# Order of the first loads, of the row statistics and of the bias product at the start of a four-layer attention kernel

## The chip, the cores and the metric

The kernel runs on one core of a Trainium2 chip. A core has a matrix engine (TensorE, PE in the profile, with its weight loads as PEld), a vector engine (VectorE, DVE), a scalar engine (ScalarE, ACT), GpSimd (POOL) and SyncE (SP), which here only issues DMAs. The metric is the device time of one execution in microseconds. The kernel before took 3056.87 us, the median of 3 runs (3055.58 to 3056.94).

## What is computed

The reference chains four layers, each a cross attention and a feed-forward part, over x (16 batches of 256 rows and 256 columns) and a context of the same shape. Only the first attention matters here:

```
def _L0_xattn_ref(query, key, value, w_q, w_k, w_v, w_o, b_q, b_k, b_v, b_o):
    q = split_heads(query @ w_q.T + b_q)
    k = split_heads(key @ w_k.T + b_k)
    v = split_heads(value @ w_v.T + b_v)
    scores = jnp.einsum('bhqd,bhkd->bhqk', q, k) / scale
    attn = jax.nn.softmax(scores, axis=-1)
    ctx = jnp.einsum('bhqk,bhkd->bhqd', attn, v)
    return ctx.transpose(0, 2, 1, 3).reshape(B, -1, D_MODEL) @ w_o.T + b_o
...
x = x + _L0_xattn_ref(_layernorm(x, axis=-1), ctx_1024, ctx_1024, ...)
x = x + _L0_ffn_ref(_layernorm(x, axis=-1), ...)
```

There are 16 heads of 16 columns. Queries come from the normalised x, keys and values from the context. The feed-forward part of this layer rounds its three weight matrices to -1, 0 and 1 after it divided them by the mean of their absolute values, so all of a matrix must have been read before it can be rounded.

## The kernel before

**Start.** x is kept in the core's memory, one tile of 128 x 2 x 256 for each batch. Lines 81 and 82 issue its 16 loads on SP. Lines 142 to 144 take the mean and the variance of every row of all 16 batches (`tile_stats`, L113 and L114, two row tiles for each batch). Then `load_pack` loads the pack w_l0a of the attention in eight parts (L99) in the order of SPECS: wq, wk, bq, bk, wv, bv, wo, bo; and the pack w_l0f of the feed-forward part in three parts of 1 MB.

**narrow_attention** serves layer 0 and layer 3. For layer 0 it first makes the reciprocal roots of all rows at once: `inv_std` (L122), a Sqrt on ScalarE and a reciprocal on VectorE, with a load of the Sqrt table, and then the table of logarithm and exponential for the rest (L172). It makes the masks (L182 to L197), clears buffers (L208), and turns the value bias into a term of the output (L211 to L221): two transposes, a copy, four matmuls with wo, and an addition into bo. That sum, `add_bias`, is added to x on GpSimd when a batch enters (L237).

**One batch.** `context` loads the transposed context (cT, 256 KB, three buffers). `values` makes the values (L290), `project` keys and queries (L261), each with a second copy by `rest_of` (L283). `enter` normalises x (L129), `turn` transposes it (L247). Batch 0 does all this before the loop. The loop then has eight half steps for each batch: in each, two heads' pairs of scores (L446 into s_ps), their row maxima on VectorE (L321), and seven half steps later the same products the other way round (t_ps), their exponentials on ScalarE (L349) and the weighted sums (L361). s_ps has three buffers and each half step takes two, so the maxima decide when TensorE can go on. The stages of the next batch are spread over these half steps: context and enter at h = 0, turn at 1, queries at 2 and 3, keys at 4 and 5, values at 7. Batches two back are divided (L379 to L387) and leave (L407, L414), with new statistics and row extremes (L538).

**Beside the loop.** `beside` calls the generator `weights` once for each half step from batch 1 on: twelve reductions of w_l0f (L502), their total (L508 to L514), then twelve steps that round it (L519 and L520 on VectorE, L521 on GpSimd). At half step 4 of batches 8, 9 and 10 it loads the packs of later layers.

**Order.** Each engine runs its instructions in a fixed order, but this order isn't simply that of the text. When the program is built, a planner takes the written order as priority and puts instructions whose inputs it reckons to be ready into holes of their engine. `issue_after` keeps ScalarE's work behind the table load. `rsqrt` (L683 to L695) is the other way to a reciprocal root: one GpSimd operation, Ln and Exp on ScalarE, and four GpSimd operations.

Of the kernel before, what the change touches and what calls it, by code (L numbers as in the profile page):

```python
# [9 lines left out]
F32 = mybir.dt.float32  # L10
# [8 lines left out]
B = 16  # L19
# [6 lines left out]

SPECS = {
    "w_l0a": [
        ("wq", 128, (2, 256)), ("wk", 128, (2, 256)), ("bq", 128, (2,)), ("bk", 128, (2,)),
        ("wv", 128, (2, 256)), ("bv", 128, (256,)), ("wo", 128, (2, 256)), ("bo", 128, (256,)),  # L30
    ],
    "w_l0f": [("wg", 128, (2, 1024)), ("wu", 128, (2, 1024)), ("wd", 128, (8, 256))],
    "w_l1a": [("gk", 128, (6, 8)), ("gb", 128, (8,)), ("os", 128, (256,))],
# [24 lines left out]
def kernel(ctx: ExitStack, tc: tile.TileContext, a: dict, out: bass.AP):  # L58
# [19 lines left out]
    nc.gpsimd.memset(eps6, 1e-6)  # L78

    X = [xp.tile([P, 2, D], F32, name=f"x{b}") for b in range(B)]  # L80
    for b in range(B):
        nc.sync.dma_start(X[b], x_v[b])

    def pool(stack, name, bufs, space=None, side=None):
        kw = {} if space is None else {"space": space}
# [31 lines left out]
        for t in range(2):  # L117
            tile_stats(mv, 2 * b + t, X[b][:, t, :])

    root = []  # L120

    def inv_std(mv):  # L122
        r = stat.tile([P, NT], F32, tag="rstd", name="rstd")
        root[:] = [nc.scalar.activation(r, mv[:, :, 1], AF.Sqrt, bias=eps5)]
        nc.vector.reciprocal(r, r)
        return r

    def normalize(dst, src, mv, r, i):
        nc.vector.tensor_scalar(dst, src, mv[:, i, 0:1], r[:, i : i + 1], ALU.subtract, ALU.mult)  # L129

# [8 lines left out]
                nc.tensor.transpose(pt[:, c, t * P : (t + 1) * P], xn[:, t, c * P : (c + 1) * P], ident)  # L139
        nc.scalar.copy(dst[:, :, dst_off : dst_off + S], pt)  # L140

    mv = new_stats()
    for b in range(B):
        batch_stats(mv, b)

    def bcast_max(col, wk, ps):

        t1 = ps.tile([1, P], F32, tag="misc", name="gm_ps")
# [7 lines left out]
        return m  # L156


    def narrow_attention(tag, w, mv, q_bias=None, k_bias=None, v_bias=None, add_bias=None,
                         new=None, rstd=None, wk=None, ps=None, before=None, between=None, beside=None, left=None, one_set=False):  # L160

        SCALE = 0.25
        with ExitStack() as st:
            one = pool(st, f"{tag}one", 1)
            if rstd is None:
                new = new_stats()
                rstd = inv_std(mv)
                if one_set:  # L170
                    with tc.issue_after(root[0].ins):
                        tables = nc.scalar.preload_act_table_set("natural_log_exp_and_others")  # L172
                    st.enter_context(tc.issue_after(tables.ins))
                wk = pool(st, f"{tag}wk", 2)
                ps = pool(st, f"{tag}ps", 2, PSUM)


            i32 = ident.rearrange("p (a b) -> p a b", b=32)
# [29 lines left out]
                nc.gpsimd.memset(t, 0.0)  # L208
            for t in vals:
                nc.gpsimd.memset(t[:, :, :, 16:17], 1.0)  # L210
            if v_bias is not None:  # L211

                bT = one.tile([P, 2, P], F32, name="bT")
                pb = ps.tile([P, 2, P], F32, tag="misc", name="bT_ps")
                for c in range(2):
                    nc.tensor.transpose(pb[:, c, :], v_bias[:, c * P : (c + 1) * P], ident)
                nc.vector.tensor_copy(bT, pb)
                pb = ps.tile([P, D], F32, tag="misc", name="bo_ps")
                for c in range(2):
                    nc.tensor.matmul(pb, lhsT=bT[:, c, :], rhs=w["wo"][:, c, :], start=(c == 0), stop=(c == 1))  # L220
                nc.vector.tensor_tensor(add_bias, pb, add_bias, ALU.add)  # L221

            state = {}

            def context(b):
                cT = wk.tile([P, 2, S], F32, tag="cT", name="cT", bufs=3)
                nc.sync.dma_start(cT, ctxT_v[b])
                state[b] = dict(cT=cT, v=vals[b % 3])

            def enter(b):  # L230

                xn = wk.tile([P, 2, D], F32, tag="xn", name="xn", bufs=3)
                for t in range(2):
                    normalize(xn[:, t, :], X[b][:, t, :], mv, rstd, 2 * b + t)
                if add_bias is not None:
                    for t in range(2):
                        nc.gpsimd.tensor_tensor(X[b][:, t, :], X[b][:, t, :], add_bias, ALU.add)  # L237
                state[b]["xn"] = xn

            def turn(b):  # L240
                s = state[b]
# [42 lines left out]

            def values(b):
                s = state[b]
                pv = ps.tile([P, 2, D], F32, tag="misc", name="v_ps")
                for t in range(2):
                    for c in range(2):
                        nc.tensor.matmul(  # L290
                            pv[:, t, :],
                            lhsT=s["cT"][:, c, t * P : (t + 1) * P],
                            rhs=w["wv"][:, c, :],
                            start=(c == 0),
                            stop=(c == 1),
                        )
                for par in range(2):
                    d_ = s["v"][:, :, :, 32 * par : 32 * par + 16].rearrange("p t h d -> p (t h) d")
                    s_ = pv.rearrange("p t (h x) -> p (t h) x", x=32)[:, :, 16 * par : 16 * par + 16]
                    nc.scalar.copy(d_, s_)  # L300
# [115 lines left out]
                if left is not None:  # L416
                    left(b, new)

            context(0)
            values(0)  # L420
            project(0, "k")
            rest_of(0, "k")
# [3 lines left out]
            turn(0)  # L426
            project(0, "q")
            rest_of(0, "q")
            if between is not None:
                between()  # L430

# [2 lines left out]
            for i in range(halves + (16 if beside is None else 40)):  # L434
                b, h = divmod(i, 8)
                made, flipped = [], []
                if i < halves:
                    made = score_mms(i // 2, i % 2)
                if 0 <= i - LAG < halves:
                    flipped = flipped_mms((i - LAG) // 2, (i - LAG) % 2)  # L440

                lists = [m for pair in zip(made, flipped) for m in pair] if made and flipped else made + flipped
                for t in range(2):
                    for _, _, mms in lists:
                        out_, l_, r_ = mms[t]
                        nc.tensor.matmul(out_, lhsT=l_, rhs=r_, start=True, stop=True)  # L446
                if made:
                    maxima(i // 2, made)
                if h == 5 and b + 1 < B:
                    rest_of(b + 1, "k")  # L450
                if flipped:
                    exps((i - LAG) // 2, flipped)
                if h % 4 == 1 and 5 <= i <= halves + 1:
                    top_rows(i // 4 - 1)
                if h % 2 == 0 and 0 <= i - LAG - 3 < halves:
                    weigh((i - LAG - 3) // 2)

                if b + 1 < B:
                    if h == 0:
                        context(b + 1)  # L460
                        enter(b + 1)
                    elif h == 1:
                        turn(b + 1)
                    elif h == 2:
                        project(b + 1, "q")
                    elif h == 3:
                        rest_of(b + 1, "q")
                    elif h == 4:
                        project(b + 1, "k")
                    elif h == 7:  # L470
                        values(b + 1)
                if h == 2 and 2 <= b <= B + 1:
                    divide(b - 2, 1)
                elif h == 3 and 2 <= b <= B + 1:
                    back(b - 2, 1)
                elif h == 6 and 2 <= b <= B + 1:
                    leave(b - 2)
                elif h == 5 and 1 <= b <= B:
                    divide(b - 1, 0)
                elif h == 7 and 1 <= b <= B:  # L480
                    back(b - 1, 0)
                if beside is not None:
                    beside(b, h, ps)
        return new


    def l0_attn(mv, w, w_f, qp, load):
        q = dict(
            wg=qp.tile([P, 2, 1024], BF16, name="l0g"), wu=qp.tile([P, 2, 1024], BF16, name="l0u"),
            wd=qp.tile([P, 8, 256], BF16, name="l0d"), deq=qp.tile([P, 3], F32, name="l0deq"),  # L490
# [5 lines left out]

        def weights(ps):

            tot = qp.tile([P, 3, 4], F32, name="l0tot")
            for j, n in enumerate(names):  # L500
                for c in range(4):
# [24 lines left out]
        def beside(b, h, ps):  # L526
            if not made:
                made.append(weights(ps))
            if h == 4 and 8 <= b < 11:
                load(("w_l1a", "w_l1f", "w_l2a")[b - 8])  # L530
            if b >= 1:
                next(made[0], None)

        def left(b, new):
# [23 lines left out]

        with ExitStack() as st:
            sp = pool(st, "l0sp", 2)  # L560
            mv = narrow_attention(
                "l0a", w, mv, q_bias=w["bq"], k_bias=w["bk"], v_bias=w["bv"], add_bias=w["bo"], beside=beside, left=left,
                one_set=True,
            )
            for _ in made[0]:
                pass
        return mv, q
# [1396 lines left out]
    with ExitStack() as st:  # L1964
        keep = pool(st, "l3keep", 1)
        dram = pool(st, "l3dram", 1, bass.MemoryType.DRAM)
        with ExitStack() as s2:
            qp = pool(s2, "l2fq", 1)
            with ExitStack() as s1:
# [2 lines left out]
                pq = pool(s_q, "l0fq", 1, side="right")  # L1972
                with ExitStack() as s0:
                    pf, pa = pool(s0, "l0fw", 1), pool(s0, "l0aw", 1)
                    wa = load_pack(pa, "w_l0a")
                    wf = load_pack(pf, "w_l0f")
                    mv, q0 = l0_attn(mv, wa, wf, pq, lambda n: packs.update({n: load_pack(pw, n, lambda z: not late(z))}))
                mv, q2 = layers_1_2(q0, s_q, qp, packs)
            xs, acc, wm, g = layers_2_3(mv, q2, keep, dram)
        l3_ffn(xs, acc, wm, g)  # L1980
# [112 lines left out]
```

## Time and profile before

| what | value |
|---|---|
| median of 3 runs | 3056.87 us |
| profiled execution, its own time | 3063.33 us |
| its span | 3061.6 us |
| TensorE busy | 2792.1 us (91%) |
| VectorE busy | 1751.6 us (57%) |
| ScalarE busy | 1282.2 us (42%) |
| GpSimd busy | 973.6 us (32%) |
| mean granted TensorE clock | 0.954 |
| first 20 us: busy TensorE, VectorE | 0.66 us, 14.62 us |
| 20 to 40 us: busy TensorE, VectorE | 11.87 us, 12.79 us |
| DMA in the first 40 us | 299 and 258 GB/s |

Times in the profile's rows count from the start of the span. A row of the chain of waits gives start, length, and engine, tile and line; it follows the work that ended last back to the start. A row of the timeline gives start, length, engine, line, operation, the tile written and the tiles read, and the count. A row of the table of stages gives the length of a stage and then each engine's busy time and count, the granted clock as a share of full speed, the busy share of the DMA engines and what they moved. A busy TensorE isn't one at its peak: a matmul at half the clock counts as longer.

### The profile page before, as it was taken

How to read it: one execution, taken by the hardware profiler on the slowest of the kernel's cores; microseconds unless marked ns; L12 is line 12 of the kernel's file. 1: busy time of each engine (PE TensorE's matmuls, PEld its weight loads, DVE VectorE, ACT ScalarE, POOL GpSimd, SP SyncE). 2: the span in 40 equal slices, each digit the busy share in tenths (PEclk: the TensorE clock that was granted, in tenths of full speed). 3: DMA queues.
4: the chain of work that ended last, by engine and by line, in shares of the span. 5: the costliest groups of instructions: out<-in, count | busy, mean ns of one | idle time of the engine just before them, and what ended most of it. 6: DMA issues, size and time to landing. Idle time of an engine off the chain costs nothing.

```text
span 3061.6 us, 49389 instructions
## 1 busy us (share of the span) xinstructions
PE 2792.1 (91%) x18661; PEld 1983.1 (65%) x18683; DVE 1751.6 (57%) x4397; ACT 1282.2 (42%) x3293; POOL 973.6 (32%) x1944
## 2 busy tenths in 40 slices
PE   5899998787999999999999998698999959999996
PEld 4566664445666666666666664355666648888885
DVE  6777676894555555555555666987777561222221
ACT  2455556664444444444444445534555531111110
POOL 1100003453433344433443333321010034555552
PEclk9899998888999999999999999889999979999998
DMA  5000000000000000000000000411010035676764
GB/s 181 15 12 12 19 1 1 15 1 31 11 11 11 11 11 11 11 11 11 11 11 5 15 18 27 155 65 44 29 32 29 22 114 170 209 216 208 215 211 118
DMA packets 81772, 177.09 MB, mean 58 GB/s; under 512 B 25935, under 2 KB 50526, under 8 KB 70590
## 3 DMA queue, kind: packets, MB, share of 16 engines
q0 software_dynamic: 24864, 105.69, 11.4%
q1 hardware_dynamic: 56670, 68.25, 7.1%
q8 instruction: 147, 2.41, 0.3%
q14 instruction: 91, 0.75, 0.1%
HBM read 147.04 MB, written 31.06 MB: 58 GB/s over the span
## 4 chain that ended last, share of the span: by engine, by line
PE 75%; DVE 11%; POOL 5%; issue 4%; ACT 3%; DMA 1%; POOLq 0%; SPq 0%; DVEq 0%; ACTq 0%
PE h_ps L1883 8%; PE o_ps L1905 8%; PE s_ps L446 7%; PE qk_ps L1038 6%; PE acc_ps L361 4%; PE acc_ps L1177 4%; PE qk_ps L261 4%; PE out_ps L1098 4%; PE s_ps L1119 3%; PE eT_ps L1161 3%; PE v_ps L1054 3%; PE t_ps L446 2%; PE v_ps L290 2%; PE out_ps L407 2%; DVE low L1128 1%
## 5 line engine op out<-in xcount | busy, mean ns | idle before, releaser
L349 ACT ACTIVATE e<-t_ps 128x512 f32<-128x512 f32 x512 | 278.2, 594 | 228.5 <-PE t_ps L446 207.4
L321 DVE TENSOR_REDUCE top<-s_ps 128x2 f32<-128x512 f32 x512 | 330.7, 682 | 50.5 <-PE t_ps L446 43.6
L1138 ACT ACTIVATE e<-s_ps,low 128x256 f32<-128x256 f32 x512 | 236.2, 472 | 288.4 <-DVE low L1128 287.8
L1149 POOL TENSOR_SCALAR e<-e,total 128x256 f32<-128x256 f32 x512 | 238.4, 485 | 325.2 <-DVE total L1146 227.4
L446 PE MATMUL s_ps<-k,q 32*128 32x256 f32 x2048 | 332.0, 411 | 10.1 <-DVE top L321 9.9
L446 PE MATMUL t_ps<-q,k 32*128 32x256 f32 x2048 | 337.4, 409 | 2.7 <-ACT e L349 2.6
L1883 PE MATMUL h_ps<-xgT,w 128*128 128x256 f32 (+1 forms) x1248 | 254.7, 362 | 0.0
L1905 PE MATMUL o_ps<-w,h 128*128 128x256 f32 x1136 | 251.6, 379 | 0.0
L446 PEld LDWEIGHTS s_ps<-k,q 32*128 32x128 f32 x2048 | 197.8, 188 | 82.7 <-issue 35.7
L1128 DVE TENSOR_REDUCE low<-s_ps 128x2 f32<-128x512 f32 x256 | 164.3, 683 | 134.7 <-PE s_ps L1119 134.7
L1883 PEld LDWEIGHTS h_ps<-xgT,w 128*128 128x128 f32 x1248 | 222.1, 192 | 27.6 <-ACT xgT L1872 0.2
L1905 PEld LDWEIGHTS o_ps<-w,h 128*128 128x128 f32 x1136 | 212.9, 190 | 27.4
L446 PEld LDWEIGHTS t_ps<-q,k 32*128 32x128 f32 x2048 | 206.0, 187 | 20.3 <-ACT e L349 14.0
L1895 ACT ACTIVATE h<-h_ps,w 128x256 f32<-128x256 f32 (+1 forms) x156 | 62.5, 451 | 370.9 <-PE h_ps L1883 361.8
L1177 PE MATMUL acc_ps<-eT,v 128*64 128x256 f32 x1024 | 172.4, 397 | 38.5 <-DVE eT L1164 38.4
L1164 DVE COPY eT<-eT_ps 128x512 f32<-128x512 f32 x256 | 165.2, 678 | 19.4 <-PE eT_ps L1161 19.3
L1893 DVE TENSOR_SCALAR h<-h_ps,w 128x256 f32<-128x256 f32 (+1 forms) x156 | 64.5, 455 | 179.1 <-PE h_ps L1883 121.2
L1915 DVE TENSOR_TENSOR y<-o_ps,w 128x256 f32<-128x256 f32 x71 | 27.1, 420 | 226.3 <-PE o_ps L1905 226.3
L1177 PEld LDWEIGHTS acc_ps<-eT,v 128*64 128x64 f32 x1024 | 70.6, 136 | 124.3 <-DVE eT L1164 67.4
L1119 PE MATMUL s_ps<-k,q 64*128 64x256 f32 x1024 | 148.3, 404 | 0.0
L361 PE MATMUL acc_ps<-e,vals 128*32 128x256 f32 x2048 | 143.6, 393 | 0.0
L1161 PE MATMUL eT_ps<-ident,e 128*128 128x128 f32 x1024 | 143.1, 285 | 0.0
(477 smaller groups left out, 5605.2 us busy)
## 6 DMA issues: line engine op xcount, KB each, us to landing
cT<-in_ctxT_dram SPq DMA_DIRECT2D x32, 256.0 KB, 2.7
away<-h SPq DMA_DIRECT2D x30, 256.0 KB, 2.0
h<-away SPq DMA_DIRECT2D x30, 256.0 KB, 3.7
x<-in_x_dram SPq DMA_DIRECT2D x16, 256.0 KB, 5.9
w_l2a<-in_w_l2a_dram SPq DMA_DIRECT2D x4, 1024.0 KB, 7.0
va<-in_ctx_dram SPq DMA_DIRECT2D x32, 128.0 KB, 2.9
c1T<-in_ctxT_dram SPq DMA_DIRECT2D x16, 256.0 KB, 2.6
c2T<-in_ctxT_dram SPq DMA_DIRECT2D x16, 256.0 KB, 2.7
```

Source lines behind the costliest of these rows:

```text
L321: nc.vector.tensor_reduce(top[:, :, col], sp, AX.X, ALU.max)
L349: nc.scalar.activation(e, tp, AF.Exp)
L361: nc.tensor.matmul(acc[32 * j : 32 * j + 32, par, :], lhsT=s["v"][:, k, 4 * g + j, 16 * par : 16 * par + 32], rhs=es[j][:, k, :], start=(k ...
L446: nc.tensor.matmul(out_, lhsT=l_, rhs=r_, start=True, stop=True)
L1119: nc.tensor.matmul(sp[j][:, t, :], lhsT=q[rows, g % 2, t * P : (t + 1) * P], rhs=k[rows, g % 2, :], start=True, stop=True,)
L1128: nc.vector.tensor_reduce(low[:, :, j], sp[j], AX.X, ALU.max, negate=True)
L1138: nc.scalar.activation(es[j][:, t, :], sp[j][:, t, :], AF.Exp, bias=low[:, t, j : j + 1], accum_out=total[:, t, j : j + 1])
L1149: nc.gpsimd.tensor_scalar(es[j][:, t, :], es[j][:, t, :], total[:, t, j : j + 1], 1.0, ALU.mult, ALU.mult)
L1161: nc.tensor.transpose(pt[:, k, t * P : (t + 1) * P], es[j][:, t, k * P : (k + 1) * P], ident)
L1177: nc.tensor.matmul(s["acc"][64 * j : 64 * j + 64, g % 2, :], lhsT=s["v"][g // 4][:, k, (2 * (g % 4) + j) * 64 : (2 * (g % 4) + j + 1) * 64 ...
L1883: nc.tensor.matmul(pp[:, f - f0, cols_], lhsT=w1[:, c * 1024 + f * P : c * 1024 + (f + 1) * P], rhs=xT[:, c, cols_], start=(c == 0), stop= ...
L1905: nc.tensor.matmul(pp[:, j, :], lhsT=h[:, f, j * P : (j + 1) * P], rhs=w2[:, f * D : (f + 1) * D], start=(f == 0), stop=(f == 7),)
```

## The change

SPECS holds w_l0a in another order. Before the loop of x loads there is now only x0; `narrow_attention` loads the first context block, then (through a function that it is handed) the pack w_l0a, then x1 to x15. Statistics of batch 0 are taken alone and its root is made by `rsqrt`; the Sqrt, its table and the reciprocal are gone. Batch 1 has its statistics and root ahead of the loop, and half step i of the loop takes those of batch i + 2; roots follow for batches 2 and 3, 4 to 9, and 10 to 15. The bias product stands behind the queries of batch 0, and `add_bias` is added to the x of batch 0 behind it. The pack w_l0f is loaded by the generator `weights` at half step 7 of batch 0. Layer 3 calls the same function; there only its first context load stands earlier in the text.

```diff
-        ("wq", 128, (2, 256)), ("wk", 128, (2, 256)), ("bq", 128, (2,)), ("bk", 128, (2,)),
-        ("wv", 128, (2, 256)), ("bv", 128, (256,)), ("wo", 128, (2, 256)), ("bo", 128, (256,)),
+        ("wv", 128, (2, 256)), ("wk", 128, (2, 256)), ("bk", 128, (2,)), ("wq", 128, (2, 256)), ("bq", 128, (2,)),
+        ("bv", 128, (256,)), ("wo", 128, (2, 256)), ("bo", 128, (256,)),
...
-    for b in range(B):
+    def load_x(b):
         nc.sync.dma_start(X[b], x_v[b])
+    load_x(0)
...
-    mv = new_stats()
-    for b in range(B):
-        batch_stats(mv, b)
...
-                new = new_stats()
-                rstd = inv_std(mv)
-                if one_set:
-                    with tc.issue_after(root[0].ins):
-                        tables = nc.scalar.preload_act_table_set("natural_log_exp_and_others")
-                    st.enter_context(tc.issue_after(tables.ins))
+                new, mv = new_stats(), new_stats()
+                rstd = stat.tile([P, NT], F32, tag="rstd", name="rstd")
+                tables = nc.scalar.preload_act_table_set("natural_log_exp_and_others")
+                st.enter_context(tc.issue_after(tables.ins))
...
+            def roots(lo, hi):
+                cols = slice(2 * lo, 2 * hi)
+                rsqrt(wk, rstd[:, cols], mv[:, cols, 1], ALU.add, 1.0, 1e-5)
+
+            context(0)
+            if fresh:
+                w = w()
+                q_bias, k_bias, v_bias, add_bias = (w[n] for n in ("bq", "bk", "bv", "bo"))
+                for b in range(1, B):
+                    load_x(b)
+                batch_stats(mv, 0)
+                roots(0, 1)
...
             project(0, "q")
             rest_of(0, "q")
+            if v_bias is not None:
...
+            biased(0)
+            if fresh:
+                batch_stats(mv, 1)
+                roots(1, 2)
...
+                if fresh and i + 2 < B:
+                    batch_stats(mv, i + 2)
+                    for lo, hi in ((2, 4), (4, 10), (10, B)):
+                        if i + 3 == hi:
+                            roots(lo, hi)
...
         def weights(ps):
+            w_f.update(load("w_l0f"))
+            yield
...
-            if b >= 1:
+            if b >= 1 or h == 7:
                 next(made[0], None)
```

The lines behind `if v_bias is not None` are those of L211 to L221, unchanged.

More of the change, by code (lines that the diff above doesn't have):

```diff
@@ L118, in batch_stats @@
             tile_stats(mv, 2 * b + t, X[b][:, t, :])
[L120 to L126, printed above, removed]
     def normalize(dst, src, mv, r, i):
@@ L156, in bcast_max, with narrow_attention @@
         return m
-    def narrow_attention(tag, w, mv, q_bias=None, k_bias=None, v_bias=None, add_bias=None,
-                         new=None, rstd=None, wk=None, ps=None, before=None, between=None, beside=None, left=None, one_set=False):
+    def narrow_attention(tag, w, mv, new=None, rstd=None, wk=None, ps=None, before=None, between=None, beside=None, left=None):
         SCALE = 0.25
@@ L166, in narrow_attention, with context @@
             one = pool(st, f"{tag}one", 1)
-            if rstd is None:
-                new = new_stats()
-                rstd = inv_std(mv)
-                if one_set:
-                    with tc.issue_after(root[0].ins):
-                        tables = nc.scalar.preload_act_table_set("natural_log_exp_and_others")
-                    st.enter_context(tc.issue_after(tables.ins))
+            q_bias = k_bias = v_bias = add_bias = None
+            fresh, state = rstd is None, {}
+            if fresh:
[3 more added lines that the diff above has]
+                st.enter_context(tc.issue_after(tables.ins))
                 wk = pool(st, f"{tag}wk", 2)
                 ps = pool(st, f"{tag}ps", 2, PSUM)
+            def context(b):
+                cT = wk.tile([P, 2, S], F32, tag="cT", name="cT", bufs=3)
+                nc.sync.dma_start(cT, ctxT_v[b])
+                state[b] = dict(cT=cT)
+            def roots(lo, hi):
[9 more added lines that the diff above has]
+                roots(0, 1)
             i32 = ident.rearrange("p (a b) -> p a b", b=32)
@@ L210, in narrow_attention @@
                 nc.gpsimd.memset(t[:, :, :, 16:17], 1.0)
[L211 to L228, printed above, removed]
             def enter(b):
@@ L234, in enter, with biased @@
                     normalize(xn[:, t, :], X[b][:, t, :], mv, rstd, 2 * b + t)
+                if b:
+                    biased(b)
+                state[b]["xn"] = xn
+            def biased(b):
                 if add_bias is not None:
@@ L237, in enter @@
                         nc.gpsimd.tensor_tensor(X[b][:, t, :], X[b][:, t, :], add_bias, ALU.add)
-                state[b]["xn"] = xn
             def turn(b):
@@ L286, in values @@
                 s = state[b]
+                s["v"] = vals[b % 3]
                 pv = ps.tile([P, 2, D], F32, tag="misc", name="v_ps")
@@ L417, in leave @@
                     left(b, new)
-            context(0)
             values(0)
@@ L428, in narrow_attention @@
             rest_of(0, "q")
+            if v_bias is not None:
+                bT = one.tile([P, 2, P], F32, name="bT")
+                pb = ps.tile([P, 2, P], F32, tag="misc", name="bT_ps")
+                for c in range(2):
+                    nc.tensor.transpose(pb[:, c, :], v_bias[:, c * P : (c + 1) * P], ident)
+                nc.vector.tensor_copy(bT, pb)
+                pb = ps.tile([P, D], F32, tag="misc", name="bo_ps")
+                for c in range(2):
+                    nc.tensor.matmul(pb, lhsT=bT[:, c, :], rhs=w["wo"][:, c, :], start=(c == 0), stop=(c == 1))
+                nc.vector.tensor_tensor(add_bias, pb, add_bias, ALU.add)
+            biased(0)
+            if fresh:
+                batch_stats(mv, 1)
+                roots(1, 2)
             if between is not None:
@@ L484, in narrow_attention, with l0_attn @@
         return new
-    def l0_attn(mv, w, w_f, qp, load):
+    def l0_attn(w, w_f, qp, load):
         q = dict(
@@ L560, in l0_attn @@
             sp = pool(st, "l0sp", 2)
[L561 to L564, printed above, removed]
+            mv = narrow_attention("l0a", w, None, beside=beside, left=left)
             for _ in made[0]:
@@ L1974, with load @@
                     pf, pa = pool(s0, "l0fw", 1), pool(s0, "l0aw", 1)
-                    wa = load_pack(pa, "w_l0a")
-                    wf = load_pack(pf, "w_l0f")
-                    mv, q0 = l0_attn(mv, wa, wf, pq, lambda n: packs.update({n: load_pack(pw, n, lambda z: not late(z))}))
+                    def load(n):
+                        if n == "w_l0f":
+                            return load_pack(pf, n)
+                        packs[n] = load_pack(pw, n, lambda z: not late(z))
+                    mv, q0 = l0_attn(lambda: load_pack(pa, "w_l0a"), {}, pq, load)
                 mv, q2 = layers_1_2(q0, s_q, qp, packs)
```

## The prediction

> **What bounds the kernel now.** I read the page first. Its chain that ended last is three quarters TensorE work and 1% DMA:
>
> ```profile
> PE 75%; DVE 11%; POOL 5%; issue 4%; ACT 3%; DMA 1%; POOLq 0%; SPq 0%; DVEq 0%; ACTq 0%
> ```
>
> So whatever comes before the first long run of matmuls is paid in full, and what is saved there is kept if nothing later waits for anything but work that has moved with it. The change touches the first 130 us only, so I read the chain of waits there (start, length, what):
>
> ```profile
> 1.81 4.69 DMA x<-in_x_dram
> ...
> 17.98 1.28 ACT L124
> ...
> 22.12 2.09 PE bo_ps L220 x4
> 24.21 4.62 issue
> 28.83 3.75 PE v_ps L290 x8
> 32.59 2.12 PE qk_ps L261 x8
> 34.73 1.02 ACT k L273 x2
> ```
>
> No projection of the attention runs before 28.83. The view calls the last hole "issue"; the timeline and the DMA view of the first 60 us name its cause:
>
> ```profile
> 10.99 5.58 SPq L99 DMA_DIRECT2D w_l0a<-in_w_l0a_dram  x8
> ...
> 16.95 1.51 SPq L99 DMA_DIRECT2D w_l0f<-in_w_l0f_dram  x3
> ...
> 18.50 1.91 SPq L227 DMA_DIRECT2D cT<-in_ctxT_dram  x3
> ...
> 24.57 7.20 DVE L502 TENSOR_REDUCE l0tot<-w_l0f 128x1 f32<-128x512 f32 x12
> ```
>
> ```profile
> cT<-in_ctxT_dram SPq DMA_DIRECT2D x4, 256.0 KB, 10.1
> ```
>
> The first context block is issued at 18.50, behind 4 MB of x, 1 MB of attention weights and 3 MB of FFN weights, and lands 10.2 us later (the tile view's longest), at 28.7: that is the start of v_ps. The first scores follow at 38.93, 10.10 us after v_ps began. The last line shows that the written order is not the executed one: those twelve reductions are written for batches 1 and 2, and were put into a hole of VectorE.
>
> Then I measured each batch, from its v_ps to the next one's, by the table of stages (columns: length, busy PE, PEld, DVE, ACT, POOL, granted clock, DMA):
>
> ```profile
> 60.67:85.73 25.06, 23.51 (x213) 15.34 (x213) 14.48 (x30) 12.64 (x26) 1.52 (x2) 0.93 0.05 12
> 85.73:111.51 25.78, 24.72 (x249) 16.84 (x247) 18.34 (x45) 13.52 (x29) 3.55 (x5) 1.00 0.05 12
> 111.51:151.25 39.74, 33.10 (x248) 19.83 (x245) 30.59 (x93) 14.30 (x30) 9.90 (x26) 0.79 0.08 21
> 151.25:176.98 25.73, 25.03 (x248) 16.56 (x244) 18.20 (x44) 13.78 (x29) 1.52 (x2) 1.00 0.05 12
> ```
>
> A steady batch is 25.73 us, of which TensorE is busy 25.03 and VectorE 18.20. The third row is the warning: there the rounding of the FFN weights and the set-up of layer 1 raise VectorE to 30.59, the clock falls to 0.79, and the batch takes 14.0 us more than a steady one.
>
> **The change, part by part.**
>
> *Loads in the order of use.* SP now issues x0, cT0, then wv, wk, bk, wq, bq, bv, wo, bo, then x1 to x15, then later contexts. By the rows, an x issue costs 9.80/16 = 0.61 us and a weight issue 5.58/8 = 0.70, so cT0 goes out at 0.80 + 0.61 = 1.4 and wv at 2.0. x0 landed 2.9 us after its issue, at 3.68; while the queue was full the DMA engines moved 334 to 392 GB/s (stages 3.68 to 18.00 and 18.00 to 28.83), or 0.67 to 0.78 us for 256 KB, so cT0 lands near 4.4 and wv near 5.2. v_ps starts there in place of 28.83: **-23.6 us**. wk (about 5.9) is in time for the keys 3.75 us later, wq (issued 4.2, landing 7.5) for the queries at 12.6. x1 is issued at 7.6 and x15 at 16.2; cT1, issued at 16.8, is wanted by the keys of batch 1, 50.30 - 38.93 = 11.4 us behind the first score, so at 26.7. With 5.5 MB ahead of it (14 to 16.5 us at those rates, and 2.9) it lands by 20. w_l0f lands behind it, by 31.
>
> *Statistics and root of batch 0.* This replaces the bound at 17.98, which had waited for 32 statistics. Two of them are done at 5.5. The root is one GpSimd operation, Ln, Exp, four more GpSimd operations; at 203.79 that series took 1.84 us from first start to last end (205.43 + 0.20 - 203.79), so 7.3, and if a first GpSimd use costs the longest of that row (1008 ns for 193) 8.2. Two normalisations of 0.37 give 8.1 to 9.0. The transposes that need them stand 34.52 - 28.83 = 5.7 us behind the start of v_ps, at 10.9: hidden, with 1.9 us of cover. The activation table loads (1.28 each) leave the path as well: one is gone, one has nothing ahead of it. So the spacing of 10.10 from v_ps to the first score stays, and the first score comes at 15.3 in place of 38.93.
>
> *Batch 1's statistics and root* come before the loop. x1 lands near 10.5; 0.8 for its statistics, 1.84 for the root and 0.74 for the normalisation give 13.9; its transposes ran 0.8 us before the first score, so 14.5. I cost it at 0; without that 0.6 us of cover it is 1 to 2 us.
>
> *Bias product.* Two transposes, a copy, four matmuls, an add. They ran in the DMA's shadow from 19.20 to 24.65 and now stand behind the queries. On TensorE they are 0.66 + 2.07 = 2.7 us at the clock of that moment. Ends: 0 (in the gap before the scores) and 5.5 (all in series). I take **+2**, near the TensorE time; the bias add on GpSimd is wanted only by the end of the batch.
>
> *Statistics of batches 2 to 15 inside the loop.* The 28 tiles after batch 1 took 6.52 to 17.89, so 0.40 us each and 0.8 per half step: 16 tiles or 6.4 us in batch 0, 12 or 4.8 in batch 1. Each waits for its x; the last lands by 20, long before its step.
>
> *FFN weights later.* The twelve reductions (7.20/12 = 0.60 each) lose their hole: 4.8 us fall in batch 1 and 2.4 in batch 2, unless they are again put ahead. What queues behind all this on VectorE is the row maxima, for which TensorE waits (score buffers come free by them). VectorE's load becomes 14.08 + 6.4 = 20.5 in batch 0 (38.93 to 64.20, 25.27 long), 14.48 + 9.6 = 24.1 in batch 1, 18.34 + 2.4 = 20.7 in batch 2. Lower end: 0, since each fits into its batch. Upper end: 11.2 + 7.2 = 18.4. Between them lie two rows: 18.34 busy cost no time, 30.59 cost 14.0. On that line 20.5, 24.1 and 20.7 cost 2.5, 6.6 and 2.7, in all 11.8. I take **+6.5**, a little over half, since free work was put into holes before, and VectorE waited 3.8 and 3.6 us on ScalarE in batch 0 alone.
>
> *Later roots* are three times two ScalarE operations of 0.2 us and five of GpSimd; with ScalarE busy 4.11 of 25.27 and GpSimd 1.51, nothing.
>
> Sum: -23.6 + 2 + 6.5 = **-15.1 us**. The profiled execution took 3063.33 for a span of 3061.6, so it would be 3048.2 with a span of 3046.5; the runs shown have a median of 3056.87, 6.5 lower, so the forecast is **3042** (3041.8).
>
> [...] The granted clock was 0.53 from 60.00 to 64.20, where eight v_ps matmuls took 3.59 us, and 1.00 from 64.20 on, where eight took 1.99: a ratio of 1.80. The clock fell when TensorE had begun to wait for VectorE's maxima, from 39 us on. [...]
>
> **Rivals.**
>
> 1. *All is hidden and the clock stays up.* For it: VectorE has 11.2 and 10.6 us free in the two batches, and batch 0 now runs at 0.73. Against it: the maxima are in its way. -23.6 - 0.27 x 25.27 = -30.4: 3026; part of it, 3030.
> 2. *The clock stays low (slower).* VectorE at 24.1 of 25.1 in batch 1 makes TensorE wait often, and the clock stays at half through batches 1 and 2. 0.80 x (23.51 + 24.72) = +38.6, so -15.1 + 38.6 = +23.5: 3080. It decides once 19 us of matmuls at full clock turn slow (15.1/0.80), a little less than one batch. For it: batch 3 now. Against it: batch 2, with weight rounding in its last 8 us, kept 1.00.
> 3. *All VectorE work is on the path*, with the bias product in series: -23.6 + 18.4 + 5.5 = +0.3: 3057.
> 4. *The order isn't as written*: loads without waits are issued early, x first. v_ps would wait for 5.5 MB, to 18: -10.8 + 8.5 = -2.3: 3055. Against it: SP's order now is the written one up to cT.
>
> **How the numbers follow.** Forecast (3035 to 3051) 0.57; rival 1, 0.15; rival 2, 0.11; rival 3, 0.12 (a quarter of it still faster); rival 4, 0.05. A measurement of this kernel can tell about 0.2%, 6.1 us, from no change. Faster: 0.57 + 0.15 + 0.03 = 0.75. Same: 0.09 + 0.05 = 0.14. Slower: 0.11. The range of 8 in 10 takes in the forecast, rival 3, rival 4 and the near part of rival 1: 3030 to 3058.
>
> **What would show it.** v_ps near 5 us and the first score near 15, no Sqrt table load, w_l0f and the l0tot reductions behind the first scores: the front is right. VectorE busy near 20, 24 and 21 us in batches 0 to 2, and the v_ps spacing 25 to 32 us: the price is right. A granted clock near 0.5 through batch 1 is rival 2. A steady batch other than 25.73, or a later layer whose length differs by some us, would mean that the executed order changed beyond the front, which I have put at nothing: then the forecast is wrong however right its steps are.

## The result

The changed kernel took 3044.0 us, the median of 5 runs (3039.1 to 3045.12), against 3056.8 for the kernel before beside it; the ratio is 0.9952, 95% interval 0.9941 to 0.9963. Run again beside the later experiments it gave 3045.08 and 0.9951 (0.9937 to 0.9965). So it is faster by about half a per cent: the medians differ by 12.8 and 13.6 us, and the two ratios stand for 14.7 and 15.0. The forecast was 3042, 14.9 below the median shown then. The profiled execution took 3044.49 for a span of 3042.8.

The chain that ended last no longer holds statistics, a table load or a hole ahead of the first scores:

```profile
1.80 4.36 DMA w_l0a<-in_w_l0a_dram
6.30 3.75 PE v_ps L284 x8
10.05 2.31 PE qk_ps L254 x8
12.38 1.02 ACT k L266 x2
13.63 0.58 ACT xT L241
14.25 2.01 PE qk_ps L254 x8
16.28 0.57 ACT q L266
16.90 0.70 PE s_ps L454 x4
17.60 1.06 PE bo_ps L431 x4
```

The first projection starts at 6.30 in place of 28.83, the first scores at 16.90 in place of 38.93. The last row is the bias product: four matmuls among the first scores. Behind them statistics of later batches (bn and mv) are on the chain, among the maxima of batch 0:

```profile
21.21 0.33 DVE bn L116
21.54 0.59 DVE top L315
22.13 0.09 DVE mv L117
22.22 0.64 DVE bn L116 x2
...
26.09 0.31 DVE bn L116
26.40 0.44 DVE q L276
26.85 0.61 DVE top L315
```

From batch 0's v_ps to batch 1's the bn and mv rows come to 3.4 us. In the next stretch, to batch 2's v_ps, the chain stays on VectorE from 45.67 to 59.63 without a break, and 5.3 us of that are reductions of w_l0f. Of the chain in these two stretches VectorE has 8.1 and 15.0 us; in the kernel before it had 4.0 and 1.8.

The rows of SP in the timeline show the new order of loads, with the FFN weights behind x:

```profile
1.80 3.75 SPq L102 DMA_DIRECT2D w_l0a<-in_w_l0a_dram  x8
...
6.18 9.62 SPq L83 DMA_DIRECT2D x<-in_x_dram  x15
...
16.18 0.34 SPq L169 DMA_DIRECT2D cT<-in_ctxT_dram  x1
...
16.93 1.82 SPq L102 DMA_DIRECT2D w_l0f<-in_w_l0f_dram  x3
```

The table of stages, cut at each batch's v_ps as for the kernel before (length, busy PE, PEld, DVE, ACT, POOL, granted clock, DMA), shows what was given back:

```profile
40.12:72.99 32.87, 28.19 (x213) 17.71 (x213) 26.13 (x66) 12.77 (x28) 5.82 (x12) 0.82 0.30 109
72.99:98.77 25.78, 24.72 (x248) 16.88 (x246) 18.34 (x45) 13.52 (x29) 3.54 (x5) 1.00 0.05 11
98.77:136.76 37.99, 32.76 (x248) 19.63 (x244) 29.68 (x93) 14.29 (x30) 10.13 (x26) 0.78 0.08 22
136.76:162.50 25.74, 25.04 (x249) 16.60 (x245) 18.21 (x44) 13.77 (x29) 1.52 (x2) 1.00 0.04 12
```

The first row stood at 25.06 us with VectorE busy 14.48; it is now 32.87 with 26.13. Its 213 matmuls keep TensorE busy for 28.19 us where it was 23.51, at a granted clock of 0.82 for 0.93: of the 7.8 us lost, 4.7 are matmuls that run longer, and the rest is TensorE waiting. The other rows are nearly those of before; the third is 1.75 us shorter. In this execution the lead over the kernel before's was 22.5 us at batch 0's v_ps (28.83 to 6.30), 20.6 at batch 1's (60.67 to 40.12), 12.7 at batch 2's (85.73 to 72.99) and 14.5 behind the rounding of the FFN weights (176.98 to 162.50).

In that stretch one bunch stands out. VectorE's rows of the timeline (start, length, line, operation, tile written and read, count):

```profile
54.70 0.72 DVE L124 TENSOR_SCALAR xn<-x,mv,rstd 128x256 f32<-128x256 f32 x2
55.34 2.45 DVE L517 TENSOR_REDUCE l0tot<-w_l0f 128x1 f32<-128x512 f32 x4
57.71 0.40 DVE L124 TENSOR_SCALAR xn<-x,mv,rstd 128x256 f32<-128x256 f32 x1
58.03 0.98 DVE L276 TENSOR_SCALAR q<-qk_ps,qmul,qadd 128x256 f32<-128x256 f32 x2
58.94 0.68 DVE L315 TENSOR_REDUCE top<-s_ps 128x2 f32<-128x512 f32 x1
```

Four reductions of w_l0f, normalisations of later batches and the second copy of the queries stand ahead of a row maximum. TensorE's own row says what that did, and the stages of 5 us show the clock behind it:

```profile
59.67 0.79 PE L454 MATMUL s_ps<-k,q 32*128 32x256 f32 x1 [3.08 <-DVE top L315]
```

```profile
55.00:60.00 5.00, 1.55 (x10) 0.74 (x12) 5.00 (x12) 1.33 (x3) 2.23 (x3) 0.89 0.14 46
60.00:65.00 5.00, 5.00 (x32) 2.65 (x29) 2.47 (x5) 1.57 (x3) 2.23 (x3) 0.50 0.00 2
```

VectorE is busy 5.00 of 5.00 us, TensorE 1.55; then TensorE is busy all the time at a granted clock of 0.50.

### The profile page after: what moved, and what is told of

Its sections match the earlier page's. It is cut to its first block, busy times and chain, and to the rows that moved or that the text cites. A ratio compares the mean times of both kernels' runs of the same rounds, so it can differ in the third digit from the quotient of the medians.

```text
span 3042.8 us, 49393 instructions
## 1 busy us (share of the span) xinstructions
PE 2786.3 (92%) x18661; PEld 1983.6 (65%) x18683; DVE 1750.7 (58%) x4396; ACT 1280.9 (42%) x3301; POOL 975.5 (32%) x1969
## 4 chain that ended last, share of the span: by engine, by line
PE 74%; DVE 11%; POOL 5%; issue 4%; ACT 3%; DMA 1%; POOLq 0%; SPq 0%; DVEq 0%; ACTq 0%
PE h_ps L1895 8%; PE o_ps L1917 8%; PE s_ps L454 7%; PE qk_ps L1050 6%; PE acc_ps L355 4%; PE acc_ps L1189 4%; PE qk_ps L254 4%; PE out_ps L1110 4%; PE s_ps L1131 3%; PE eT_ps L1173 3%; PE v_ps L1066 3%; PE t_ps L454 2%; PE v_ps L284 2%; PE out_ps L401 2%; DVE low L1140 1%
```

## The experiments

The yardstick is the start of each batch's v_ps, as above: "first stretch" is from batch 0's to batch 1's, "second" from batch 1's to batch 2's. The question was first how much of the changed kernel each part makes, and then what makes the second stretch long: the amount of VectorE work in it (A), or its place in bunches ahead of the maxima, with the clock behind it (B).

**The changed kernel once more.**

> The changed kernel itself, beside the others on the same chip: 0.994 to 0.996 of the kernel before; batch 0's v_ps to batch 2's within 0.5 us of 66.69, if the front repeats from execution to execution.

Ratio 0.9951 (0.9937 to 0.9965), as expected. The two stretches took 31.75 and 32.00, 63.75 in all, and not within 0.5 us of 66.69: one kernel's front differs by 3 us between executions. So a difference of 3 us or less in these two stretches of a single profile says nothing below. The rounding repeats well: 37.99 and 37.88.

**e7: the old order of loads alone.**

```diff
+            if fresh:
+                for b in range(1, B):
+                    load_x(b)
+                w = w()
             context(0)
...
+                        w = load_pack(pa, "w_l0a")
+                        wf.update(load_pack(pf, "w_l0f"))
...
-            w_f.update(load("w_l0f"))
```

SPECS has its old order again.

> The changed kernel with the old order of loads alone: 16 x, the attention weights in the old order, the three FFN weights, and then the first context; statistics, roots and bias product as changed. If the order of loads is the whole gain of the front, batch 0's v_ps comes at 28 to 29 us in place of 6.30, and the time is that of the kernel before or up to 6 us more, since the later work keeps its cost: 3056 to 3066. Rival: the FFN weights are there early, their twelve reductions run in the hole ahead of v_ps as before, and batch 1 gets its 7 us back: 3050 to 3056.

3061.72 beside 3061.6: ratio 1.0004 (0.9992 to 1.0017). The chain of waits holds the old hole, now by its name:

```profile
19.62 8.78 DMA cT<-in_ctxT_dram
28.40 3.76 PE v_ps L285 x8
```

The stretches are 31.46 and 25.02, those of the kernel before, and the twelve reductions run in a row from 22.69 to 30.16 again, before the first score. The time is in the forecast range, and the rival had a part of the mechanism right (batch 1 gets its time back). Statistics, roots and bias product in their new places, without the loads, are worth nothing that can be measured.

**e3: the statistics ahead of the loop.**

```diff
-                batch_stats(mv, 1)
-                roots(1, 2)
+                for b in range(1, B):
+                    batch_stats(mv, b)
+                roots(1, B)
...
-                if fresh and i + 2 < B:
-                    batch_stats(mv, i + 2)
```

> The changed kernel with the statistics and roots of batches 1 to 15 written ahead of the loop again; loads, bias product and FFN weights as in the changed kernel. If statistics in the loop only cost by volume, the first two stretches keep their sum (33.82 + 32.87 = 66.69 us from batch 0's v_ps to batch 2's) within 2 us: the first grows by 3 to 6, the second shrinks by as much. If it is where they stand among the maxima that costs, the sum falls to 60 to 64, since they then run while x arrives and no maximum is behind them. Rival: the last x lands near 19 us, its statistics stand ahead of batch 0's first maxima, and the sum grows to 70 or more: then the move into the loop earned its place.

3047.41, ratio 0.9957 (0.9942 to 0.9973), which overlaps the changed kernel's. The stretches became 41.90 and 25.13, 67.03 in all: the sum didn't move (66.69 and 63.75), though the split did, by 8 us where 3 to 6 had been expected. From 18.7 to 26.8 the statistics stand in front of batch 0's first maximum in this kernel, and the second stretch has none. So in these two batches the statistics cost the same in both places, as A says; since they stand in rows ahead of maxima in both, this doesn't speak against B. With e7 this splits the change: the order of loads makes the gain, and moving the statistics into the loop neither adds nor costs anything that can be measured.

**e8: the bias product ahead of the values.**

```diff
+            if v_bias is not None:
+                bT = one.tile([P, 2, P], F32, name="bT")
...
             values(0)
             project(0, "k")
...
-            if v_bias is not None:
...
```

> The changed kernel with the bias product ahead of the values again. wo lands last of the attention's weights, near 9 us: if the product holds TensorE's queue until then, v_ps starts at 9 to 10 in place of 6.30 and all after it is 2 to 4 us later. If the planner puts the values ahead of it all the same, nothing changes by more than 1 us. The prediction costed its place behind the queries at 2 us; the trace of the changed kernel shows 1.06.

v_ps started at 11.16, 4.9 us later and behind the 9 to 10 expected, since the bias product's transposes (8.12) and four matmuls (from 9.30) now ran ahead of it; the first scores came at 21.32, for 16.90. Yet batch 2's v_ps came at 72.89 (72.99 and 69.61 in the two executions of the changed kernel), and the one time is 3046.97. A delay of 4.9 us at the first projection is not seen two batches later beyond the 3 us by which that point varies. What limits these two batches is then not TensorE's start alone.

**e1 and e2: VectorE work left out.**

```diff
e1   tot = qp.tile([P, 3, 4], F32, name="l0tot")
e1 + nc.gpsimd.memset(tot, 25.0)
e1 - nc.vector.tensor_reduce(tot[:, j, c : c + 1], ...)
e2 + nc.gpsimd.memset(mv[:, 4:, 0:1], 0.0)
e2 + nc.gpsimd.memset(mv[:, 4:, 1:2], 1.0)
e2 - batch_stats(mv, i + 2)
```

> The changed kernel without the twelve reductions of w_l0f (their result is a constant; the output is not the reference's). In the changed kernel the stretch from batch 1's v_ps to batch 2's (40.12 to 72.99) takes 32.87 us, in the kernel before 25.06. Theory A (volume: a batch loses what VectorE's work in it exceeds its free time by): 7.2 us of work leave, the stretch becomes 25.7 to 26.5. Theory B (place: four reductions in a row, 55.34 to 57.79, keep TensorE waiting until its clock falls, and this costs most of the 7.8): the stretch becomes 25 to 26 and the granted clock stays at 1.00 from 50 us on. Rival C (the statistics inside the loop make the loss): it stays above 30.

> The changed kernel without the statistics of batches 2 to 15 (mean 0 and variance 1 in their place; the output is not the reference's); 11.2 us of VectorE work leave. Theory A (volume): some 6 us leave the stretch 16.90 to 40.12 and 4.5 the stretch 40.12 to 72.99, so this one comes to 28 or 29. Theory B (place): the reductions still stand in a row in front of the maxima, and the stretch stays within 2 us of 32.87. Rival C (statistics): it falls to 25 or 26. The stretch from the first score to batch 1's v_ps (23.22 us, 21.74 before) should fall to 20 to 22 by A and C.

e1: 30.14 + 29.42 = 59.56, 4.2 to 7.1 us less than the changed kernel's two executions for 7.2 us of work taken out. The second stretch stays at 29.42, between the 26 of A and B and the 30 of C. Its chain holds no statistics; it goes through the root of batches 10 to 15, which waits for the last statistics on VectorE and stands ahead of an exponential on ScalarE. e2: 35.49 + 25.29 = 60.78, 3.0 to 5.9 less for 11.2 us; the second stretch falls to 25.29 with the reductions present, as C said and not as B did.

The times, one execution each, are 3043.28 and 3047.70, and don't show what the front gained. In e2, e4 and e5 the stretch of a later layer between the first matmuls into two of its tiles, hs_ps and y_ps, takes 66.7 to 67.0 us, in the changed kernel and the kernel before 63.2 and 63.3; why isn't known. For e2 alone that is 3.8 us.

VectorE's timeline of e2 shows nine reductions in the second stretch, which begins near 41, seven of them in a row among the maxima:

```profile
41.58 0.68 DVE L317 TENSOR_REDUCE top<-s_ps 128x2 f32<-128x512 f32 x1
42.18 4.23 DVE L518 TENSOR_REDUCE l0tot<-w_l0f 128x1 f32<-128x512 f32 x7
46.33 1.28 DVE L317 TENSOR_REDUCE top<-s_ps 128x2 f32<-128x512 f32 x2
```

A longer bunch than the changed kernel's four, and the stretch is as short as in the kernel before: a bunch need not cost time. But this one runs beside the v_ps matmuls (40.99 to 44.46), which wait for no maximum, and isn't on the chain; the changed kernel's four are. So a bunch that does hold up maxima isn't tested by it. The sum of both stretches goes roughly with VectorE's work in them; the split between the two isn't explained by it.

**e4, e5: work kept behind the maxima.**

```diff
+                    top_of[:] = [nc.vector.tensor_reduce(top[:, :, col], sp, AX.X, ALU.max)]
...
+                with tc.issue_after(top_of[0].ins):
                     next(made[0], None)
e5 +                with tc.issue_after(top_of[0].ins):
                         batch_stats(mv, i + 2)
```

> The changed kernel with the same work, but each step of the FFN weights (twelve reductions, the totals, twelve rounding steps) kept behind the row maxima of the half step it is written for, so that it can't be put ahead in bunches. Theory A (volume): batch 1's stretch still takes 31 to 33 us, since the work is the same, and batch 3's 38. Theory B (place): batch 1's stretch falls to 26 to 28, the rounding loses part of its 12 us (38 falls to 28 to 34), and the time falls by 8 to 15 us below the changed kernel's 3044, to 3029 to 3036. Rival: spread out, the steps make TensorE wait a little in every half step and give the same loss.

> As e4_tied_weights, and the statistics of batches 2 to 15 are kept behind the maxima of their half step too. Theory B (place): as that run or up to 2 us better, if the statistics that stand in a row around 40 us delay a maximum; 3 us worse, if they were in free time and are now in the way. Theory A: no difference to the changed kernel beyond 2 us.

e4: 3034.69, ratio 0.9925 (0.9907 to 0.9942). In the first two batches almost nothing: 33.26 + 30.39 = 63.65, as in the second execution of the changed kernel. There B falls for the reductions: without a bunch of them the loss is the same. It isn't settled for the statistics, which are not held back here; they have 3.4 us of the chain's first stretch, as in the changed kernel. The second stretch also has a new holder, the root of batches 10 to 15, which ScalarE's exponentials wait for as in e1. The gain is in the rounding:

```profile
95.12:121.48 26.36, 25.35 (x248) 16.68 (x244) 24.41 (x60) 13.78 (x29) 6.45 (x11) 1.00 0.04 11
121.48:151.83 30.35, 27.81 (x248) 17.64 (x244) 24.31 (x80) 13.87 (x30) 5.41 (x20) 0.94 0.11 28
```

Two batches take 56.7 us, 63.7 in the changed kernel, and the clock stays at 1.00 and 0.94 (0.78 there). VectorE is busy 48.7 us in them, 47.9 there: the work is the same and only its place differs. There B holds. e5: 3039.87, 0.9938 (0.9926 to 0.9951), with 31.32 + 34.13 in front. With the statistics kept behind the maxima, a normalisation at 46.88 waits 3.49 us for the root of six batches, which runs on GpSimd from 43.48 to 46.84; neither theory had that, and the time fits neither. The intervals of e4 and e5 overlap.

**e9: the statistics spread as well.**

```diff
-                if fresh and i + 2 < B:
-                    batch_stats(mv, i + 2)
+                if fresh and b + 2 < B and h in (1, 3):
+                    with tc.issue_after(top_of[0].ins):
+                        tile_stats(mv, 2 * b + 4 + h // 2, X[b + 2][:, h // 2, :])
+                    if h == 3:
+                        roots(b + 2, b + 3)
```

> The changed kernel with every step of the FFN weights kept behind the maxima of its half step (as in e4_tied_weights) and the statistics of batch b + 2 taken in half steps 1 and 3 of batch b, one tile each, behind the maxima, with a root for each batch. Theory B (place and bunches): the first stretch falls to 31 to 32 us and the second to 26 to 28 (33.26 and 30.39 in e4_tied_weights), the rest as there, so the time is 4 to 6 us below that run's 3034.7, at 3028 to 3031. Theory A (volume, and the slow clock of batch 0 stays): less than 2 us.

3033.63, ratio 0.9915 (0.9901 to 0.9928): below the changed kernel's interval, and by time not to be told from e4: 1.1 us, as A said. The front is 4.1 us shorter, 32.97 + 26.61 = 59.58, as B said of the second stretch. The statistics that left these batches stand in later ones, two tiles each, and the batch of 25.95 us that follows is a steady one's length within 0.3.

**e6 and e10: the FFN weights two batches later.**

```diff
-            if b >= 1 or h == 7:
+            if b >= 3 or (b, h) == (2, 7):
```

> The changed kernel with the FFN weights' steps two batches later and nothing kept behind the maxima. If the place of the reductions in the text decides, batch 1's stretch falls from 32.87 us to the 29.4 of e1_no_totals. If the planner puts them ahead into batch 1 all the same, since w_l0f is there, it stays at 31 to 33 and the four-in-a-row is seen again before 60 us. Loading w_l0f at the end of batch 2 in the text may delay them by itself.

> As e9_spread, but the steps of the FFN weights begin two batches later, so the reductions fall in batches 3 and 4 and the rounding in 4 to 6. If the reductions in batch 1 still cost something when spread (26.61 us there, 25.06 in the kernel before), that stretch falls to 25.1 and batches 3 and 4 take at most 0.5 us more each: 1 us below e9_spread's 3033.6. If a steady batch (18.20 of 25.73 us VectorE) has less room than batch 1, the reductions cost 1 to 3 us there and the time is the same or up to 3 us longer. The rounding's own loss (the stretches of 27.47 and 30.30) should stay, since it moves as a whole.

e6, from the changed kernel, kept its second stretch at 31.92, and one time was 3050.73. The reductions are written for batches 3 and 4, but the planner puts all twelve into batch 1 (the first starts at 48.12). These are seven of them in VectorE's timeline:

```profile
48.12 1.26 DVE L517 TENSOR_REDUCE l0tot<-w_l0f 128x1 f32<-128x512 f32 x2
...
51.29 1.86 DVE L517 TENSOR_REDUCE l0tot<-w_l0f 128x1 f32<-128x512 f32 x3
...
54.86 1.26 DVE L517 TENSOR_REDUCE l0tot<-w_l0f 128x1 f32<-128x512 f32 x2
```

The four in a row are gone, and the stretch is as long, as in e4. e10, from e9, has the reductions where they are written:

```profile
36.39:61.87 25.48, 24.32 (x213) 15.81 (x213) 15.39 (x34) 12.92 (x28) 2.48 (x7) 0.92 0.39 141
61.87:87.17 25.30, 24.99 (x246) 16.72 (x245) 16.97 (x40) 13.68 (x31) 2.49 (x7) 1.00 0.03 12
87.17:113.67 26.50, 25.55 (x248) 16.84 (x244) 22.84 (x55) 13.99 (x31) 2.42 (x7) 1.00 0.03 11
113.67:140.21 26.54, 25.71 (x251) 17.24 (x247) 23.31 (x59) 13.99 (x31) 3.29 (x9) 1.00 0.03 11
```

The first two stretches take 29.84 + 25.48 = 55.32, within 3 us of the 56.90 of the kernel before: with the added work gone from them, their loss is gone. The reductions, and the few statistics beside them, cost 0.8 us in each of the two steady batches that now hold them (26.50 and 26.54 beside 25.73), for 4.6 and 5.1 us of VectorE work. 3033.12, ratio 0.9912 (0.9896 to 0.9928): the lowest median, and not to be told from e9. Both beat both kernels.

## Why the prediction was right, point by point

**The front: -23.6 forecast, -22.5 measured.** v_ps came at 6.30 and not at 5.2. Its last input was the weights' transfer, 4.36 us from issue to landing, where the prediction took x0's 2.9 us from issue to landing and a place in a moving queue behind it. e7, which has all of the change but the loads' order, has the hole again.

**Issue times.** SP issued the eight weight loads in 3.75 us, 0.47 each, not 0.70; in the kernel before it spent 0.33 to 0.34 us on each and stood idle between them, so the row of before contained waits. x1 went out at 6.18, not 7.6. This harmed nothing.

**Root of batch 0.** Taken as 1.84 us; in the trace it runs from 4.67 to 8.28, 3.61 us, because buffer clearing on GpSimd (rows of 0.56, 0.74, 0.73 and 0.73 us) stands between its operations. VectorE then waited 1.13 us for batch 1's x, to 9.76, before it came to batch 0's normalisation, which ended at 11.15; the transposes started at 12.18. The cover of 1.9 us shrank to 1.0 and held.

**First score.** 10.60 us behind v_ps, not 10.10: 16.90 for a forecast of 15.3.

**Batch 1's root at 0.** Right: it was done at 14.82 and its transposes ran at 21.13. The later roots, put at nothing too, aren't on the changed kernel's chain in these batches; in e1, e4 and e5 one of them holds up work there.

**Bias product: +2 forecast.** 1.06 us on the chain and two transposes in the gap before (16.08). Half of the estimate, though e8 warns that 5 us at this place need not show at the end.

**VectorE's work in the loop: +6.5 forecast.** The first stretch grew by 1.98 (1.06 of it the bias product), the second by 7.81, the batch behind by 0.00, and the rounding got 1.75 shorter, 8.0 in all with the bias product, where the prediction had 8.5. In the second execution it was 5.0 (-0.09 + 6.94 + 0.01 - 1.86). The line between the two rows gave 2.5, 6.6 and 2.7 for the three batches; the third was 0.00, since all twelve reductions ran ahead: one in batch 0, eleven in batch 1.

So the sum came out near, and partly by luck. The line was halved because the planner would put work into holes. What it did was to pull work ahead into the first two batches, and these lost 8.7 us without the bias product, more than the 6.5 (5.8 in the second execution). The shorter rounding, which no term had, gave 1.75 of it back. Of the prediction's own signs for the price, VectorE was to be busy near 20, 24 and 21 us: from v_ps to v_ps it was 26.61, 26.13 and 18.34. The spacing was to be 25 to 32 us: it was 33.82 and 32.87 here, and 31.75 and 32.00 in the second execution.

What makes the loss is VectorE's added work: it stands on the chain of waits, and in e10, where most of it is moved to later batches, the loss is gone. How the amount sets the size is argued and not shown. In the kernels that ran, the sum of the two stretches goes roughly with VectorE's busy time in them, one execution each but for the changed kernel (e8 lies lowest for its work, e10 ran below the kernel before):

| kernel | VectorE busy, us | both stretches, us |
|---|---|---|
| before | 32.6 | 56.9 |
| e7 | 33.1 | 56.5 |
| e10 | 35.5 | 55.3 |
| e9 | 39.4 | 59.6 |
| e2 | 43.0 | 60.8 |
| e1 | 45.7 | 59.6 |
| e4 | 49.7 | 63.7 |
| e5 | 49.9 | 65.5 |
| e8 | 50.5 | 61.7 |
| changed, two executions | 52.7 and 52.1 | 66.7 and 63.8 |
| e6 | 52.7 | 65.8 |
| e3 | 53.4 | 67.0 |

Against the kernel before, the changed kernel's two executions have 20.1 and 19.5 us more of VectorE work for 9.8 and 6.9 us more of time, 0.49 and 0.35 us for each; e10's steady batches paid 0.16 to 0.17. So it isn't the amount alone: the price is higher where VectorE already sets the pace. In these two batches place moved the split, and hardly the sum.

**Rival 2, the clock.** It came in part. The granted clock is 0.82 over batch 1 (0.93 before) and 0.50 between 60 and 65 us. The longer matmuls, 4.7 us, are inside the 7.81 and not on top of it; in the second execution they are 3.6 of 6.9. The prediction's line had such a cost in it, since its upper row ran at 0.79. The clock did not stay low into batch 2 (1.00), so the rival's 38.6 us did not come.

**The rest of the kernel** was put at nothing. A steady batch is 25.74 us, as before. The prediction called itself wrong if a later layer's length differed by some us. In the profiled executions the lead is 14.5 us at 162.50 and 18.8 at the end. Of that drift 3.7 us come in one place, between the first matmuls into two tiles of later layers, eT_ps and wT_ps: 999.11 us there, 1002.76 in the kernel before. In the second execution of the changed kernel it is 1002.54. So one kernel's executions differ by this much, and it isn't the change. The medians differ by 12.8, since the kernel before's profiled execution took 3063.33 and its other runs at that time 3055.58 to 3056.94. What makes an execution longer stays open.

## What to carry to other kernels

Order the first loads by first use before anything else: here that made the gain, and it could be read from one hole in the chain of waits and one landing time. Work that had lost its hole wasn't free in the loop here, though VectorE had been busy only 18.15 of 31.84 us and 14.48 of 25.06 us in the kernel before's two stretches; look for the stretch in which that engine will set the pace, and spread the work over batches in which it has room. The first two batches lost 0.35 to 0.49 us for each us of added work, the steady ones 0.16 to 0.17. Where a planner orders the instructions, look for what it pulls ahead: a position in the text did not hold the reductions back, an explicit order behind the maxima did. That took the kernel to 3034.7, some 10 us below the changed one; with the statistics spread as well it took 3033.1 and 3033.6, which can't be told from 3034.7.

## What the runs showed of the hardware

In the two falls shown here the granted clock went to 0.50 behind waits of TensorE no longer than 2.00 us. In the changed kernel the fall came in the microsecond from 28.00. Between its first matmul at 6.30 and there, the longest wait was 1.65 us, ahead of this row:

```profile
27.50 1.49 PE L454 MATMUL s_ps<-k,q 32*128 32x256 f32 x4 [1.65 <-DVE top L315]
```

```profile
26.00:27.00 1.00, 0.00 (x0) 0.00 (x0) 1.00 (x5) 0.00 (x0) 0.00 (x0) 1.00 1.04 434
27.00:28.00 1.00, 0.50 (x2) 0.47 (x3) 1.00 (x3) 0.00 (x0) 0.00 (x0) 1.00 0.96 395
28.00:29.00 1.00, 1.00 (x4) 0.32 (x3) 1.00 (x3) 0.00 (x0) 0.00 (x0) 0.57 0.98 380
29.00:30.00 1.00, 1.00 (x3) 0.82 (x4) 1.00 (x5) 0.00 (x0) 0.00 (x0) 0.50 0.92 294
```

It then stayed at 0.50 until 45 us, with TensorE busy all the time from 30 us on:

```profile
30.00:35.00 5.00, 5.00 (x17) 3.10 (x15) 2.08 (x8) 1.33 (x4) 1.54 (x5) 0.50 0.44 102
35.00:40.00 5.00, 5.00 (x26) 3.52 (x24) 4.90 (x11) 0.60 (x1) 0.48 (x2) 0.50 0.03 0
40.00:45.00 5.00, 5.00 (x21) 3.55 (x24) 4.33 (x14) 1.24 (x3) 0.45 (x1) 0.50 0.02 4
45.00:46.00 1.00, 1.00 (x14) 0.57 (x6) 0.35 (x1) 0.31 (x1) 0.00 (x0) 0.90 0.72 211
```

In the kernel before, batch 111.51 to 151.25 has such a fall. Its clock fell between 118 and 119 us (0.77 there, 1.00 ahead of it), and its longest wait ahead of that was 2.00 us:

```profile
118.02 0.48 PE L446 MATMUL s_ps<-k,q 32*128 32x256 f32 x1 [2.00 <-DVE top L321]
```

Both waits, of 1.65 and 2.00 us, stand among short runs of scores. What makes the clock fall or return, and when, these runs don't show. What they do show is the price in one stretch: of the 7.8 us that the changed kernel's batch 1 lost, 4.7 are matmuls that ran longer, at a granted clock of 0.82 for 0.93, and 3.1 are waits of TensorE.
